# A fused attention and mixture-of-experts block on one core: row blocks turned by VectorE, expert weights split by ScalarE, gates folded into the shared expert, and another order at the end

## The chip, the cores and the metric

The kernel runs on one core of a Trainium2 chip as one launch. Its metric is the device time in microseconds; lower is better. A profile of one execution shows the engines by these names: PE (TensorE, with its weight loads as PEld), DVE (VectorE), ACT (ScalarE), POOL (GpSimd) and SP (SyncE, which issues most of the DMAs).

## The reference

Everything is float32. There are 32 sequences of 256 tokens with 128 features, 8192 tokens in all. Each sequence `b` has its own shift, scale and gate rows.

```
h = layernorm(x) * (1 + ca[b]) + sa[b]
x = x + ga[b] * attention(h)            # 16 heads of 64, softmax over the queries
h = layernorm(x) * (1 + cb[b]) + sb[b]
x = x + gb[b] * (routed(h) + shared(h) + 0.1 * anchor(h))
```

- `routed`: 32 experts of width 64 in 4 groups of 8. Every token takes the two groups with the highest group scores, and in them its 6 best experts; an expert computes `silu(h @ wg) * (h @ wu) @ wd`, weighted by the token's own weight for it.
- `anchor`: 16 small experts of width 32, four to a group; the token's best expert says which of them counts.
- `shared`: one expert of width 64 for all tokens.

## The kernel before

**Attention (the first 860 us).** The tokens are cut into 16 chunks of 512. A hand-written table says at which of the attention steps each portion of a chunk's norms and routing is dealt out. `through_dram` with `load_blocks` (L386 to L402) turns a normalized chunk: it is written to DRAM and read back in four DMAs of 32 columns each, after which one DVE transpose of 32x32 blocks (L652) completes the turn. Routing writes every token's row to DRAM twice, once for each of its two groups, by indirect DMAs of POOL (`route_send`, L850). A row is `ROW` = 180 floats: 128 features and 52 floats of weights.

**The passage to the experts (860 to 900 us).** SP issues the loads for the first expert tiles (`fetch_rows` for three tiles, `fetch_weights` for two, L1371 to L1374). Then a loop over seven pairs of chunks (L1379) computes the shared expert: `shared_up` (L1292) on PE, ACT and DVE, and one round later `shared_down` (L1305), whose two PSUM results are copied to `h2_all`, one by ACT and one by DVE. Between the rounds the routing of the last two chunks goes on, which takes DVE and POOL.

**The experts (900 to 1384 us).** There are 35 tiles of 512 tokens, each of one group. A tile `j` has five steps `k`: four pairs of routed experts and one step for the four anchors. In a step, `up` (L1237) does two PE products of 128x512 (`pg`, `pu`), `silu` on ACT and two DVE products, the first with `pu` and the second with the spread token weights `bt`; `down` (L1250) follows one step later with the product by `wd_sb` or `ad_sb` into one PSUM tile `py` for the tile. After a tile `send` (L1273) copies `py` on ACT and scatters it by four indirect DMAs of POOL to `y_d` in DRAM.

What a tile needs is prepared ahead by instructions dealt out between the steps (L1411 to L1420), in the program's order on every queue:

- `fetch_rows(j + 3)` and `fetch_weights(j + 2)` at `k == 0`: SP reads the tile's group and row from a table, and issues one DMA of rows and four of weights;
- `weights_mine(j + 2)` at `k == 1` on DVE; `weights_turn(j + 2)` at `k == 2`: a PE transpose (`pc`), an ACT copy (`cwt`), and on SP the DMA to DRAM (`cd`), followed at once by six DMAs that spread it over the partitions (`bt`, five slices of 512 columns);
- `rows_turn(j + 1)` at `k == 3`: four PE transposes (`ph`, L1233) and an ACT copy to `h`.

**The last sums.** When all of a chunk's tiles have been sent, `pass_load` (L1328) at `k == 4` loads its two shares and its gate row on SP. `pass_sum` four steps later adds the shares and the shared expert on DVE and multiplies by the gate on POOL; `pass_out` three steps after that adds `x1` and writes the chunk. The last shared pair is done inside the expert loop (L1429 to L1434). What is left over after the last tile runs at the end (L1443 to L1451); the last chunk goes there in two halves (`pass_rest`).

A tile waits in program order on its queue: an engine or SP that waits for one instruction does nothing that stands behind it.

Of the kernel before, what the change touches and what calls it, by code (L numbers as in the profile page):

```python
# [56 lines left out]
def adaln_block_kernel(  # L57
# [80 lines left out]
    def late_loads():  # L138

        nc.sync.dma_start(out=wd_sb, in_=w_down.rearrange("(k p) m -> p k m", p=P))  # L140
        nc.sync.dma_start(out=ad_sb, in_=an_down.rearrange("(k p) m -> p k m", p=P))
        nc.sync.dma_start(out=sg_sb, in_=sh_gate)
        nc.sync.dma_start(out=su_sb, in_=sh_up)
        for h in range(P // SI):
            nc.sync.dma_start(out=sd_sb[h * SI : (h + 1) * SI], in_=sh_down)
# [174 lines left out]
    with ExitStack() as actx:  # L320
# [516 lines left out]
        def route_write(c):  # L837

            w, ws, one = (chunk[c].pop(k) for k in ("w", "ws", "one"))
            meta = chunk[c]["rows"][:, :, D:].rearrange("p i (g w) -> p i g w", w=GW)  # L840
            wk = w.rearrange("p i (g k q) -> p i g k q", g=NG, q=2)
            for q in range(2):
                nc.gpsimd.tensor_tensor(
                    meta[:, :, :, q * EPG // 2 : (q + 1) * EPG // 2], wk[:, :, :, :, q],
                    ws.unsqueeze(2).unsqueeze(3).to_broadcast([P, NT, NG, EPG // 2]), ALU.mult,
                )
            pair = one.rearrange("p t (g l e) -> p t g l e", g=NG, e=2)
            nc.gpsimd.tensor_tensor(
                meta[:, :, :, EPG : GW - 1], pair[:, :, :, :, 0], pair[:, :, :, :, 1], ALU.add
            )  # L850
# [298 lines left out]
        fin = actx.enter_context(tc.tile_pool(name="fin", bufs=3, reuse_waits="tile"))  # L1149
# [9 lines left out]
        def fetch_rows(j):  # L1159
            t = T[j]  # L1160
            of, n = t["of"]
            t["g_sp"] = nc.sync.value_load(of.table[0:1, 0, n : n + 1], min_val=0, max_val=NG - 1)
            r = nc.sync.value_load(of.table[0:1, 1, n : n + 1], min_val=0, max_val=NG * SPAN)
            t["rw"] = rwp.tile([P, NT, ROW], F32, tag="rw", name=f"rw_{j}")
            got = nc.sync.dma_start(
                out=t["rw"],
                in_=rows_d[bass.ds(r, CH), :].rearrange("(p i) f -> p i f", i=NT),
            )
            if j < FIRST:
                tc.declare_no_dep(  # L1170
                    got.ins, group="late rows", reason="this tile holds rows of earlier chunks"
                )
                tc.add_to_no_dep_group("first tiles", got.ins)

        def fetch_weights(j):
            t = T[j]
            g = t.pop("g_sp")
            for key, src, srca in (("wg", w_gate, an_gate), ("wu", w_up, an_up)):
                w = wp.tile([P, KU + 1, P], F32, tag=key, name=f"{key}_{j}")
                nc.sync.dma_start(  # L1180
                    out=w[:, 0:KU, :].rearrange("p k f -> p (k f)"),
                    in_=src[:, bass.ds(g * (KU * P), KU * P)],
                )
                nc.sync.dma_start(out=w[:, KU, :], in_=srca[:, bass.ds(g * P, P)])
                t[key] = w

        def weights_mine(j):

            t = T[j]
            of, n = t["of"]  # L1190
            mm = mp.tile([P, NT, NG, GW], F32, tag="mm", name=f"mm_{j}", bufs=1)
            nc.vector.tensor_tensor(
                mm,
                t["rw"][:, :, D:].rearrange("p i (g w) -> p i g w", w=GW),
                of.mine[:, n, :].unsqueeze(1).unsqueeze(3).to_broadcast([P, NT, NG, GW]),
                ALU.mult,
            )
            m = mp.tile([P, GW, NT], F32, tag="m", name=f"m_{j}")
            nc.vector.tensor_reduce(m, mm.rearrange("p i g w -> p w i g"), AX.X, ALU.add)
            ix = mp.tile([P, NT], U32, tag="ix", name=f"iy_{j}", bufs=5)  # L1200
            nc.vector.tensor_copy(ix, m[:, GW - 1, :])
            t.update(m=m, ix=ix)

        def weights_turn(j):
# [10 lines left out]
            bt = bcp.tile([P, KU + 1, CH], F32, tag="bt", name=f"bt_{j}")  # L1215
            for q in range(2):
                nc.sync.dma_start(
                    out=bt[q * EI : (q + 1) * EI, 0:KU, :],
                    in_=cd[q * KU : (q + 1) * KU].partition_broadcast(EI),
                )  # L1220
            for q in range(NG):
                nc.sync.dma_start(  # L1222
                    out=bt[q * LI : (q + 1) * LI, KU, :],
                    in_=cd[2 * KU + q].partition_broadcast(LI),
                )
            t["bt"] = bt

        def rows_turn(j):
            t = T[j]
            rw = t.pop("rw")  # L1230
            ph = ps_mm.tile([P, CH], F32, tag="mm", name=f"ph_{j}")
            for i in range(NT):
                nc.tensor.transpose(ph[:, i * P : (i + 1) * P], rw[:, i, 0:D], ident)  # L1233
            t["h"] = mp.tile([P, CH], F32, tag="h", name=f"h_{j}", bufs=2)
            nc.scalar.copy(t["h"], ph)

        def up(j, k):  # L1237
            t = T[j]
            pg, pu = (
                ps_sc.tile([P, CH], F32, tag="sc", name=f"{n}_{j}_{k}") for n in ("pg", "pu")  # L1240
            )
            nc.tensor.matmul(pg, t["wg"][:, k, :], t["h"], start=True, stop=True)  # L1242
            nc.tensor.matmul(pu, t["wu"][:, k, :], t["h"], start=True, stop=True)  # L1243
            a = hid.tile([P, CH], F32, tag="a", name=f"a_{j}_{k}")
            nc.scalar.activation(a, pg, AF.Silu)  # L1245
            nc.vector.tensor_mul(a, a, pu)  # L1246
            nc.vector.tensor_mul(a, a, t["bt"][:, k, :])  # L1247
            return a

        def down(j, k, a):  # L1250
            t = T[j]
            of, n = t["of"]
            if k == 0:
                t["g"] = nc.tensor.value_load(
                    of.table[0:1, 0, n : n + 1], min_val=0, max_val=NG - 1
                )
                t["py"] = (
                    ps_av.tile([P, NT, D], F32, tag="av", name=f"py_{j}")
                    if j % 2
                    else ps_wo.tile([P, NT, D], F32, tag="po", name=f"py_{j}")  # L1260
# [6 lines left out]
            for i in range(NT):  # L1267
                nc.tensor.matmul(  # L1268
                    t["py"][:, i, :], a[:, i * P : (i + 1) * P], w,
                    start=k == 0 and i == 0, stop=k == KU and i == NT - 1,  # L1270
                )

        def send(j):  # L1273
            t = T[j]
            y = yp.tile([P, NT, D], F32, tag="y", name=f"y_{j}")
            nc.scalar.copy(y, t.pop("py"))  # L1276
            ix = t.pop("ix")
            for i in range(NT):
# [10 lines left out]
                tc.add_to_no_dep_group("y", sent.ins)  # L1289


        def shared_up(n):  # L1292
# [10 lines left out]
            return n, a  # L1303

        def shared_down(n, a, banks):  # L1305
# [5 lines left out]
            for i in range(NT):  # L1311
                for h in range(2):
# [6 lines left out]
                    )  # L1319
            for h, c in enumerate(cs):  # L1320
                (nc.scalar.copy, nc.vector.tensor_copy)[h](
                    h2_all[c], py[h].rearrange("p i d -> p (i d)")
                )
# [4 lines left out]
        def pass_load(c):  # L1328
            t = S_[c]
            t["s"] = [  # L1330
                xin.tile([P, NT, D], F32, tag="xt", name=f"s{k}_{c}") for k in range(2)
            ]
            for k, s in enumerate(t["s"]):
                o = k * B * S + c * CH
                got = nc.sync.dma_start(
# [3 lines left out]
            t["gate"] = fin.tile([P, BPC, D], F32, tag="gate", name=f"gate_{c}")  # L1339
            nc.sync.dma_start(  # L1340
                out=t["gate"],
                in_=gate_dram[c * BPC : (c + 1) * BPC].partition_broadcast(P),
            )

        def pass_sum(c):
            s0, s1 = S_[c]["s"]
            nc.vector.tensor_add(s0, s0, s1)
            nc.vector.tensor_add(s0, s0, h2_all[c].rearrange("p (i d) -> p i d", d=D))
            for b in range(BPC):
                nc.gpsimd.tensor_tensor(  # L1350
# [3 lines left out]
        def pass_rest(c, b):  # L1354
# [4 lines left out]
            nc.vector.tensor_add(  # L1359
                s0, s0, h2_all[c].rearrange("p (i d) -> p i d", d=D)[:, part]  # L1360
            )
# [17 lines left out]
        for n in range(PAIRS):  # L1379
# [12 lines left out]
            if n == 3:  # L1392
                weights_turn(1)
            if n == 4:
                rows_turn(0)
        shared_down(*prev, two_banks)
# [5 lines left out]
        prev = pair = None  # L1402
        for j in range(LISTS):
            for k in range(KU + 1):
                a = up(j, k)
                if prev is not None:
                    down(*prev)
                    if prev[1] == KU:
                        send(j - 1)
                prev = (j, k, a)  # L1410
# [6 lines left out]
                if k == 2 and j + 2 < LISTS:  # L1417
                    weights_turn(j + 2)
                if k == 3 and j + 1 < LISTS:
                    rows_turn(j + 1)  # L1420

# [7 lines left out]
                elif pair is None:  # L1429
                    assert FIRST - 3 > j  # L1430
                    pair = shared_up(PAIRS)
                elif len(pair) > 1:
                    shared_down(*pair, ((ps_mm, "mm"), (ps_mm, "mm")))
                    pair = (PAIRS,)  # L1434
# [3 lines left out]
                if k == 4 and started < NCH and complete[started] <= j:  # L1438
                    pass_load(started)
                    due[j + 1, 3] = lambda c=started: pass_sum(c)  # L1440
                    due[j + 2, 1] = lambda c=started: pass_out(c)
                    started += 1
        down(*prev)  # L1443
        send(LISTS - 1)
        for at in sorted(due):
            due[at]()
        for c in range(started, NCH):
            pass_load(c)
# [54 lines left out]
```

## Time and profile before

| | |
|---|---|
| median of 14 runs | 1406.59 us (1403.69 to 1411.37) |
| the profiled execution | 1405.5 us, of which 1403.7 us span |
| PE busy | 1349.7 us, 96% |
| DVE busy | 1015.8 us, 72% |
| ACT busy | 798.3 us, 57% |
| POOL busy | 767.6 us, 55% |
| mean granted TensorE clock | 0.988 |

The profile's page gives each engine's busy time, the span in 40 slices, and a chain of waits that is followed back from the last instruction. Further views give the instructions in order of time, the waits, and the busy time of each engine in a stretch. Busy times of an engine are averages over stages with different limits, so each stage is read by itself. Matmul durations are modelled from pipelined records: two that follow each other closely overlap in the list, so the distance between starts is the cost of one.

### The profile page before, as it was taken

The page shows a single profiled execution, that of the slowest core. Times are in us where ns is not written, and L with a number is a line of the kernel's source. Part 1 is how long each engine was busy: PE and PEld are TensorE (multiplying, and loading weights), DVE is VectorE, ACT ScalarE, POOL GpSimd, SP SyncE. Part 2 cuts the span into 40 slices and gives each one's busy share as a digit, 9 for nine tenths or more (in the row PEclk, how much of TensorE's full clock was granted, in tenths as well). Part 3 has the DMA queues.
Part 4 walks back from the last instruction along what each step waited for, and adds up shares of the span by engine and source line. Part 5 has one row for each costly group of instructions (what it writes and reads, how often), then busy time and mean ns, then how long its engine had stood idle before and what let it go on. Part 6 is the DMA issues. An engine that isn't in the chain of part 4 may idle for free. (4 is left out here: it accounts for less than half of the span.)

```text
span 1403.7 us, 33682 instructions
## 1 busy us (share of the span) xinstructions
PE 1349.7 (96%) x10543; PEld 841.6 (60%) x10543; DVE 1015.8 (72%) x4277; ACT 798.3 (57%) x2767; POOL 767.6 (55%) x1294
## 2 busy tenths in 40 slices
PE   6999999999999999999999998899999999999994
PEld 2566666666666666666666665456666666666662
DVE  5666888888888878888877776576656567766664
ACT  4777777777777777777777774223333333333331
POOL 3536467767767767767867646344323234343333
PEclk9999999999999999999999999999999999999997
DMA  4773622122022022022032014767667778878772
GB/s 154 275 264 116 221 75 50 42 75 62 31 75 62 30 75 62 30 75 62 31 75 47 33 48 118 191 175 214 179 181 199 193 206 231 266 223 256 227 210 63
DMA packets 183599, 182.50 MB, mean 130 GB/s; under 512 B 81520, under 2 KB 142656, under 8 KB 178944
## 3 DMA queue, kind: packets, MB, share of 16 engines
q1 hardware_dynamic: 172112, 159.62, 41.0%
q0 software_dynamic: 10624, 20.21, 4.3%
q8 instruction: 86, 1.41, 0.4%
q14 instruction: 89, 0.73, 0.2%
q10 hardware_dynamic: 688, 0.53, 0.1%
HBM read 121.37 MB, written 59.70 MB: 129 GB/s over the span
## 5 line engine op out<-in xcount | busy, mean ns | idle before, releaser
L549 ACT ACTIVATE e<-e,mn 128x256 f32<-128x256 f32 (+1 forms) x1024 | 453.5, 445 | 198.5 <-DVE mn L539 197.7
L539 DVE CUSTOM_DVE_ANT_0 e<-psc,mask 128x256 f32<-128x256 f32 (+1 forms) x1024 | 304.8, 344 | 4.4 <-PE psc L518 1.2
L1279 POOL DMA_INDIRECT y_d<-y,iy x140 | 137.9, 985 | 240.6 <-ACT y L1276 208.3
L568 POOL TENSOR_TENSOR vs<-v,rc 128x256 f32<-128x256 f32 x256 | 151.9, 616 | 212.0 <-DVE rc L557 199.9
L518 PEld LDWEIGHTS psc<-q,k 64*128 64x128 f32 x2048 | 166.2, 187 | 113.4 <-issue 101.6
L1246 DVE TENSOR_TENSOR a<-a,pu 128x512 f32<-128x512 f32 x175 | 120.1, 686 | 146.9 <-PE pu L1243 146.7
L1245 ACT ACTIVATE a<-pg 128x512 f32<-128x512 f32 x175 | 104.5, 597 | 183.0 <-PE pg L1242 174.9
L518 PE MATMUL psc<-q,k 64*128 64x256 f32 (+1 forms) x2048 | 202.1, 336 | 0.0
L586 PE MATMUL pav<-e,vs 128*64 128x256 f32 (+1 forms) x2048 | 195.1, 333 | 5.7 <-POOL vs L568 5.7
L549 ACT ACTIVATION_READ_ACCUMULATOR e<-e,mn 128x1 f32 x1024 | 192.7, 188 | 0.0
L1268 PEld LDWEIGHTS py<-wd_sb,a 128*128 128x128 f32 x1120 | 146.9, 192 | 70.3 <-issue 46.2
L1242 PE MATMUL pg<-h,wg 128*128 128x512 f32 x350 | 180.6, 598 | 0.0
L1243 PE MATMUL pu<-h,wu 128*128 128x512 f32 x350 | 179.6, 595 | 0.0
L468 PEld LDWEIGHTS po<-wo_sb,z 128*64 128x64 f32 x2048 | 121.8, 138 | 70.2 <-issue 69.7
L586 PEld LDWEIGHTS pav<-e,vs 128*64 128x64 f32 x2048 | 127.0, 136 | 58.5 <-POOL vs L568 6.4
L489 DVE TENSOR_SCALAR q<-pq,negbq 128x512 f32<-128x512 f32 x128 | 95.9, 749 | 76.9 <-PE pq L468 75.3
L856 POOL DMA_INDIRECT rows_d<-rows,ix x128 | 130.2, 1017 | 37.4 <-issue 34.6
L1268 PE MATMUL py<-wd_sb,a 128*128 x1120 | 148.2, 275 | 1.4 <-DVE a L1247 1.4
L479 DVE TENSOR_TENSOR v<-pv,bv_sb 128x512 f32<-128x512 f32 x128 | 88.3, 689 | 81.1 <-PE pv L468 79.7
L468 PE MATMUL po<-wo_sb,z 128*64 128x128 f32 x2048 | 134.7, 274 | 0.0
L468 PE MATMUL pq<-n_t,wqkv_sb 128*64 128x512 f32 x512 | 133.4, 600 | 0.7 <-ACT n_t L302 0.7
L468 PE MATMUL pv<-wqkv_sb,n_t 128*64 128x512 f32 x512 | 132.3, 596 | 0.8 <-DVE q L489 0.5
(239 smaller groups left out, 1770.6 us busy)
## 6 DMA issues: line engine op xcount, KB each, us to landing
bt<-cd SPq DMA_DIRECT2D x70, 512.0 KB
rows_d<-blank SPq DMA_DIRECT2D x69, 360.0 KB
rw<-rows_d SPq DMA_DIRECT2D x35, 360.0 KB
wg<-in_w_gate_dram SPq DMA_DIRECT2D x35, 256.0 KB
wu<-in_w_up_dram SPq DMA_DIRECT2D x35, 256.0 KB
bt<-cd SPq DMA_DIRECT2D x140, 64.0 KB
s<-y_d SPq DMA_DIRECT2D x32, 256.0 KB
mb<-mod_dram SPq DMA_DIRECT2D x31, 256.0 KB
```

The lines of the kernel that those rows point to most:

```text
L468: nc.tensor.matmul(ps[r], a[:, r], b, start=start, stop=stop)
L518: nc.tensor.matmul(pb[h][:, cols], k[r, o + kb * P : o + (kb + 1) * P], q[r, o + kb * P : o + S], start=True, stop=True,)
L539: nc.vector.tensor_tensor_reduce(e[:, cols], ps[:, cols], mask[:, cols], 1.0, 3e38, ALU.add, ALU.min, mn[:, b, kb, h : h + 1],)
L549: nc.scalar.activation(e[:, cols], e[:, cols], AF.Exp, bias=mn[:, b, kb, h : h + 1], scale=-1.0, accum_out=sm[:, b, kb, h : h + 1],)
L568: nc.gpsimd.tensor_tensor(vs[:, 2 * b : 2 * b + 2], vt[:, 2 * b : 2 * b + 2, col : col + P].rearrange("p k (h d) -> p k h d", h=2), rc[:, ...
L586: nc.tensor.matmul(pav[h * DH : (h + 1) * DH, o + kb * P : o + S], vs[:, 2 * b + kb, h, :], e[:, 0 : 2 * P] if kb == 0 else e[:, 2 * P : 3 ...
L856: sent = nc.gpsimd.indirect_dma_start(out=rows_d[:, :], out_offset=bass.IndirectOffsetOnAxis(ap=ix[:, k, i : i + 1], axis=0), in_=rows[:, ...
L1242: nc.tensor.matmul(pg, t["wg"][:, k, :], t["h"], start=True, stop=True)
L1243: nc.tensor.matmul(pu, t["wu"][:, k, :], t["h"], start=True, stop=True)
L1246: nc.vector.tensor_mul(a, a, pu)
L1268: nc.tensor.matmul(t["py"][:, i, :], a[:, i * P : (i + 1) * P], w, start=k == 0 and i == 0, stop=k == KU and i == NT - 1,)
L1279: sent = nc.gpsimd.indirect_dma_start(out=y_d[:, :], out_offset=bass.IndirectOffsetOnAxis(ap=ix[:, i : i + 1], axis=0), in_=y[:, i, :], in ...
```

## The change

- **Rows.** `fetch_rows` issues five DMAs in place of one: the 52 floats of weights, and the features in four blocks of 32 columns (`load_blocks`). `rows_turn` is one DVE transpose; the four PE transposes and the ACT copy are gone.
- **Weights.** The routed weights are loaded as they lie (`raw`), and `split_weights`, two ACT copies of 128x512 for each tile at `k == 2` and `k == 3`, put every fourth column together. With that the token weights of all four routed steps are the same slice, and `bt` has two slices in place of five.
- **Spread.** The DMAs to `bt` (five in place of six) are a function of their own, `weights_spread`, at `k == 4`.
- **Gates.** `shared_down` no longer copies: DVE multiplies each PSUM result by the gate row in two halves, and POOL adds it to `x1`. `shared_up` loads two gate rows on SP for it. `pass_sum` no longer adds the shared part, and the gate product (`pass_gate`) runs on DVE; the three steps of a chunk's last pass stand one tile later.
- **End.** The last tile is computed in two halves of 256 tokens, each sent by itself; the last shared pair comes behind the last tile; the last chunk's two loads are issued by ACT.

```diff
         def fetch_rows(j):
...
-            t["rw"] = rwp.tile([P, NT, ROW], F32, tag="rw", name=f"rw_{j}")
-            got = nc.sync.dma_start(
-                out=t["rw"],
-                in_=rows_d[bass.ds(r, CH), :].rearrange("(p i) f -> p i f", i=NT),
-            )
+            t["rw"] = rwp.tile([P, NT, ROW - D], F32, tag="rw", name=f"rw_{j}")
+            t["rh"] = rwp.tile([P, CH // BLK, BLK], F32, tag="rh", name=f"rh_{j}")
+            rows = rows_d[bass.ds(r, CH), :]
+            got = [
+                nc.sync.dma_start(
+                    out=t["rw"], in_=rows[:, D:].rearrange("(i p) f -> p i f", p=P)
+                ),
+                *load_blocks(t["rh"], rows),
+            ]
...
         def fetch_weights(j):
...
-                w = wp.tile([P, KU + 1, P], F32, tag=key, name=f"{key}_{j}")
+                raw = wp.tile([P, P, KU], F32, tag=f"{key}r", name=f"{key}r_{j}")
                 nc.sync.dma_start(
-                    out=w[:, 0:KU, :].rearrange("p k f -> p (k f)"),
+                    out=raw.rearrange("p f k -> p (f k)"),
                     in_=src[:, bass.ds(g * (KU * P), KU * P)],
                 )
-                nc.sync.dma_start(out=w[:, KU, :], in_=srca[:, bass.ds(g * P, P)])
-                t[key] = w
+                a = wp.tile([P, P], F32, tag=f"{key}a", name=f"{key}a_{j}")
+                nc.sync.dma_start(out=a, in_=srca[:, bass.ds(g * P, P)])
+                t[key] = raw, a
+
+        def split_weights(j, key):
+            t = T[j]
+            raw, a = t[key]
+            w = wp.tile([P, KU, P], F32, tag=key, name=f"{key}_{j}", bufs=2)
+            nc.scalar.copy(w, raw.rearrange("p f k -> p k f"))
+            t[key] = [w[:, k, :] for k in range(KU)] + [a]
...
-            bt = bcp.tile([P, KU + 1, CH], F32, tag="bt", name=f"bt_{j}")
-            for q in range(2):
-                nc.sync.dma_start(
-                    out=bt[q * EI : (q + 1) * EI, 0:KU, :],
-                    in_=cd[q * KU : (q + 1) * KU].partition_broadcast(EI),
-                )
+            t["cd"] = cd
+
+        def weights_spread(j):
+            t = T[j]
+            cd = t.pop("cd")
+            bt = bcp.tile([P, 2, CH], F32, tag="bt", name=f"bt_{j}")
+            nc.sync.dma_start(
+                out=bt[:, 0, :], in_=cd[0:EPG].unsqueeze(1).to_broadcast([EPG, P // EPG, CH])
+            )
             for q in range(NG):
...
         def rows_turn(j):
             t = T[j]
-            rw = t.pop("rw")
-            ph = ps_mm.tile([P, CH], F32, tag="mm", name=f"ph_{j}")
-            for i in range(NT):
-                nc.tensor.transpose(ph[:, i * P : (i + 1) * P], rw[:, i, 0:D], ident)
             t["h"] = mp.tile([P, CH], F32, tag="h", name=f"h_{j}", bufs=2)
-            nc.scalar.copy(t["h"], ph)
+            nc.vector.transpose(t["h"], t.pop("rh").rearrange("p x r -> p (x r)"))
...
+        def load_gate(c):
+            gate = fin.tile([P, BPC, D], F32, tag="gate", name=f"gate_{c}")
+            nc.sync.dma_start(
+                out=gate,
+                in_=gate_dram[c * BPC : (c + 1) * BPC].partition_broadcast(P),
+            )
+            return gate
...
-            return n, a
+            return n, a, [load_gate(c) for c in cs]
...
             for h, c in enumerate(cs):
-                (nc.scalar.copy, nc.vector.tensor_copy)[h](
-                    h2_all[c], py[h].rearrange("p i d -> p (i d)")
-                )
+                o = h2_all[c].rearrange("p (i d) -> p i d", d=D)
+                for b in range(BPC):
+                    nc.vector.tensor_tensor(
+                        tokens(o)[:, b], tokens(py[h])[:, b], by_batch(gates[h])[:, b], ALU.mult
+                    )
+                nc.gpsimd.tensor_tensor(x1_all[c], x1_all[c], o, ALU.add)
...
         def pass_sum(c):
             s0, s1 = S_[c]["s"]
             nc.vector.tensor_add(s0, s0, s1)
-            nc.vector.tensor_add(s0, s0, h2_all[c].rearrange("p (i d) -> p i d", d=D))
+
+        def pass_gate(c):
+            s0 = S_[c]["s"][0]
             for b in range(BPC):
-                nc.gpsimd.tensor_tensor(
+                nc.vector.tensor_tensor(
...
         for j in range(3):
             fetch_rows(j)
         for j in range(2):
             fetch_weights(j)
...
             if n == 3:
                 weights_turn(1)
+                weights_spread(0)
             if n == 4:
+                weights_spread(1)
                 rows_turn(0)
+            if n == 5:
+                split_weights(0, "wg")
+                split_weights(0, "wu")
...
         for j in range(LISTS):
-            for k in range(KU + 1):
-                a = up(j, k)
+            parts = [slice(0, NT)] if j < LISTS - 1 else [slice(0, NT // 2), slice(NT // 2, NT)]
+            for k, part in ((k, part) for part in parts for k in range(KU + 1)):
+                a = up(j, k, part)
...
+                if k in (2, 3) and j + 1 < LISTS:
+                    split_weights(j + 1, ("wg", "wu")[k - 2])
                 if k == 3 and j + 1 < LISTS:
                     rows_turn(j + 1)
+                if k == 4 and j + 2 < LISTS:
+                    weights_spread(j + 2)
...
-                elif pair is None:
-                    assert FIRST - 3 > j
-                    pair = shared_up(PAIRS)
-                elif len(pair) > 1:
-                    shared_down(*pair, ((ps_mm, "mm"), (ps_mm, "mm")))
-                    pair = (PAIRS,)
...
                     pass_load(started)
-                    due[j + 1, 3] = lambda c=started: pass_sum(c)
-                    due[j + 2, 1] = lambda c=started: pass_out(c)
+                    due[j + 2, 0] = lambda c=started: pass_sum(c)
+                    due[j + 2, 2] = lambda c=started: pass_gate(c)
+                    due[j + 2, 4] = lambda c=started: pass_out(c)
                     started += 1
+
+        pair = shared_up(PAIRS)
         down(*prev)
-        send(LISTS - 1)
+        send(LISTS - 1, prev[2])
+        shared_down(*pair, ((ps_mm, "mm"), (ps_mm, "mm")))
+        for c in range(started, NCH):
+            pass_load(c, nc.scalar)
         for at in sorted(due):
             due[at]()
-        for c in range(started, NCH):
-            pass_load(c)
```

Besides, `up`, `down` and `send` take the part of the tokens that they work on; routing writes its eight weights by one POOL product in place of two; the pool of gate rows has five buffers in place of three, and the shares have a pool of six buffers of their own.

## The prediction

> **What bounds the kernel now.** I read the busy time by stretches first, then the chain of waits, SP's queue in order of time, and the end. The stretches (length; busy us and instructions of each engine; clock; DMA share, GB/s):
>
> ```profile
> core 0: us, PE busy (x) PEld busy (x) DVE busy (x) ACT busy (x) POOL busy (x), PEclk, DMA share, GB/s
> 867.00:885.44 18.44, 17.36 (x150) 9.10 (x148) 17.00 (x75) 7.60 (x16) 9.12 (x24) 1.00 0.69 185
> 885.44:899.65 14.21, 8.46 (x47) 5.00 (x46) 7.39 (x20) 2.60 (x5) 5.26 (x7) 0.90 0.79 181
> 1000.00:1050.00 50.00, 50.00 (x240) 32.29 (x239) 29.45 (x49) 16.25 (x31) 14.79 (x16) 1.00 0.64 171
> 1252.00:1350.00 98.00, 94.39 (x448) 60.02 (x447) 65.01 (x108) 30.09 (x55) 38.26 (x40) 1.00 0.84 241
> 1375.00:1404.00 29.00, 8.25 (x43) 5.47 (x41) 11.37 (x20) 2.38 (x4) 9.49 (x10) 0.73 0.24 72
> ```
>
> In the experts PE is never idle from 1000 to 1250 us, and loses 3.6 us from 1252 to 1350. In the passage (867 to 885) DVE is busy for 92%. The chain shows one step of a tile and the transposes `ph` inside it:
>
> ```profile
> 1196.99 0.89 PE py L1268 x8
> 1197.88 0.44 PE ph L1233 x4
> 1198.32 0.86 PE pg L1242 x2
> 1199.18 0.86 PE pu L1243 x2
> 1200.04 0.89 PE py L1268 x8
> ```
>
> A step costs 0.86 + 0.86 + 0.89 = 2.61, a tile 5 x 2.61 + 0.44 (`ph`) + 0.11 (`pc`) = 13.60. SP's queue, at the start of the experts and late in them:
>
> ```profile
> 862.12 4.26 SPq L1165 DMA_DIRECT2D rw<-rows_d  x3
> 866.57 0.33 SPq L1180 DMA_DIRECT2D wg<-in_w_gate_dram  x1
> 867.09 0.33 SPq L1184 DMA_DIRECT2D wg<-in_an_gate_dram  x1
> ...
> 1226.31 0.45 SPq L1214 DMA_DIRECT2D cd<-cwt  x1
> 1230.68 1.10 SPq L1217 DMA_DIRECT2D bt<-cd  x2
> 1231.84 1.97 SPq L1222 DMA_DIRECT2D bt<-cd  x4
> 1235.24 0.32 SPq L1340 DMA_DIRECT2D gate<-gate_dram  x1
> 1238.23 0.35 SPq L1165 DMA_DIRECT2D rw<-rows_d  x1
> 1241.38 0.45 SPq L1214 DMA_DIRECT2D cd<-cwt  x1
> ```
>
> Late, SP needs 15.07 us from one `cd` to the next, more than PE's 13.60: it falls behind, `pass_sum` then waits for its shares in front of the steps' products, and that is where the 3.6 us go. The end:
>
> ```profile
> 1382.85 1.16 PE L1268 MATMUL py<-ad_sb,a 128*128 x8 [0.76 <-DVE a L1247]
> 1389.18 0.97 POOL L1279 DMA_INDIRECT y_d<-y,iy  x1 [0.30 <-issue]
> 1392.83 0.94 SPq L1335 DMA_DIRECT2D s<-y_d  x2
> 1399.63 0.43 DVE L1363 TENSOR_TENSOR s<-s,x 128x256 f32<-128x256 f32 x1
> ```
>
> **1. Rows turned by DVE: -15.0.** PE loses 0.44 a tile. Of 35 groups the first (876.63) lies in the passage, so 34 x 0.44 = 15.0. In exchange DVE gets one block transpose (L652: 0.71) at `k == 3`. A step's two products take 1.38 of DVE's 2.61; the extras are now at most one of 0.69 (`k == 0`, `k == 4`), 1.05 (`mm`, `m`, `iy`), 0.86 (gates, 2 x 0.43) or 0.71 a step. The fullest step is 1.38 + 1.05 = 2.43, so PE hides all of it; without that cover it would cost 0.71 a tile, 24 us in all.
>
> **2. Weights split by ACT: 0.** ACT loses the copy of `h` (0.59) and gets two copies of 128x512 that read every fourth float. No ACT row reads so. From below: the plain copy, 0.59. From above: DVE's strided reduction L1199, 0.51 for 208 elements, 1.26 for 512. I take 0.6 to 0.85, nearer to the row of the same engine. At `k == 2` ACT then holds 0.60 (`silu`) + 0.26 (`cwt`) + the copy; even 1.26 makes 2.12 of 2.61 and delays the next `silu` by some 0.7, against 0.9 between the end of a step's products and `down` (1364.01 to 1364.94). Beyond 1.5 us the excess counts twice a tile.
>
> The Trainium skill ("SBUF — State Buffer", at "Door 1: The DMA port swizzle") speaks against this copy: full speed needs consecutive hits in a 16-byte line, and this one takes a new line with each float. It gives no price; twice 0.59 would leave the sum as it is.
>
> **3. Shared pair out of the loop: -3.0.** Its products pushed two steps apart by 1.87 (993.57 to 995.44) and 1.09 (998.25 to 999.34).
>
> **4. The passage: +12.0.** SP, not the arithmetic, decides here. `fetch_rows` three times issues 12 more DMAs ahead of the weights, 0.52 each as the weight loads are spaced: +6.2, so the first weight goes out at 872.8 instead of 866.6. The eight weight loads take 4.2 more, to 877.0. Only then come the new gate rows of pair 0, landing at about 879.5 (2 to 2.5 us, as `hb_ln`, issued to 895.2 and used at 897.79). DVE meets the product with this gate where it copied `sy` at 867.00, and everything behind it waits: the next pair's `silu` product, routing of chunks 14 and 15, and PE, whose two banks stay full. POOL waits too: its adds stand ahead of chunk 13's last four sends. That is +12.5 (bounds +9 and +15, by the landing).
>
> Then DVE sets the pace up to the first `pg` (885.44): 17.00 busy, less 6 copies of 0.69, plus 24 gate products at 0.36 (L628, from PSUM: 0.71 for two), plus 0.71 for the first transpose, gives 22.2, at the old 92% to 95% about 23.5 instead of 18.44: +5.
>
> Given back: behind the first `pg` PE stood still for 5.75 us for the logits of chunk 15, since `hd_ln` (888.15) was queued behind `bt`; and the clock was 0.90 in that stretch, a pair of `pg` taking 2.08 instead of 1.02. In the new order SP is past `bt` by then, and what is left is POOL's chain: six adds of about 1.42 each (twice L383's 0.71) ahead of chunk 15's norm. I put the rest of the stall at 2: -3.5 there, -2 for the slow matmuls. 12.5 + 5 - 3.5 - 2 = +12.0; bounds +5 and +18.
>
> On the clock, the Trainium skill ("TensorE: Matmul & The Clock Gate", Part 1: The HAM clock gate) says that an idle window of some 3.4 us halves it for as long again. By it the new hole costs half of 3.4, an estimate of 1.7 us, beneath DVE's rounds; no part of the sum uses it.
>
> **5. Stalls late in the experts: -3.6, and SP: +1.5.** `pass_sum` stands two steps and a tile after its load instead of four steps, 15.7 us instead of 10.4, so its waits go. What is late next is SP's cycle: four more row DMAs (+2.1), one large spread fewer (-0.58): 15.07 becomes 16.6 with the same 4.37 from `cd` to `bt`. That wait was 1.49 at 1046.09, when DMA was idler. The spread falls from 1280 to 512 KB a tile, the row blocks move as many features as before; at 860 us, with such blocks, the DMA moved 205 GB/s at a share of 0.95, against 388 at 1208. So I take 2.2, a cycle of 14.4, nearer to the idle row. Against PE's 13.16 that is 1.2 a tile over the eleven tiles in a row that load shares, 13.6, less some 2 us of SP's idle time and 7.5 us of lead (15.7, less 2.2 from the step to the issue and 6 for landing, `s` in the chain: 6.17): 4 at worst, nothing at a cycle of 14; I take 1.5.
>
> **6. The end: -3.5.** Two sends behind the last product instead of four: 2 x 1.28 = 2.6. ACT issues the two loads without SP's wait for chunk 14's output (0.5); each half is added with three products instead of four, 2 x 0.43. Against it: the last pair's `sg` and `su` (1.87) stand before the last `down`, of which some 1.3 were waiting time: +0.5. Its five DVE products, two adds behind the sends on POOL, and two chunks' last passes (2 x 2.2 on DVE) end before the last shares land, 3.5 after their issue; if not, they cost up to 2. In the half tiles a step has 1.31 on PE, DVE 0.85: hidden. Routing's one POOL product less a chunk lies beside attention, as does the new order of `wd_sb` in its load: 0.
>
> **Sum.** -15.0 - 3.0 + 12.0 - 3.6 + 1.5 - 3.5 = -11.6: 1393.9 against the profiled 1405.5, which is 1.1 below the median; as a median 1395.0, own range 1389 to 1402.
>
> **Rivals.**
> - *The gates are no hold-up* (17%): they land before DVE asks, or the stalls behind absorb the shift; the passage costs nothing. 1383. For it: the 5.75 us of idle PE. Against it: the order on SP.
> - *SP becomes the bound, slower than before* (11%): the place is the eleven tiles from the seventeenth on, the price 16.6 - 13.16 = 3.4 a tile, 37 less 9.5 of lead: 1395 - 1.5 + 28 = 1421.5. It decides from a cycle of 15.4 (`cd` to `bt` 3.2). For it: that wait was 4.37. Against it: 768 KB a tile less.
> - *The strided copy is slow* (5%): at 1.7 us, 0.2 x 2 x 34 = 13.6: 1409.
> - *The change doesn't do what it says* (7%): DVE's transpose makes `a` late, 0.2 a tile: 1402.
> - Forecast: 60%.
>
> Faster by over 0.2% (about what a measurement can tell from no change): 60 + 17 + 5 = 0.82; within it 0.06; slower 0.12. From 1381 to 1407 some 17% is left out.
>
> **What would show it.** Starts of `py` 13.16 apart per tile between 1000 and 1200; PE idle for some 13 us near 868 to 881, DVE there waiting for the DMA of `gate`; first `pg` near 903; `cd` to `cd` below 14.5 late; the strided copy at 0.6 to 0.85; two sends and loads on ACT's queue at the end. I am wrong where DVE does not wait for the gate, or PE waits for `bt`, the shares or the split weights.

## The result, and the profile after

The changed kernel takes 1418.04 us (median of 11 runs, 1413.12 to 1420.04) against 1409.32 us of the kernel before (median of 52 runs): ratio 1.0063, 95% interval 1.0051 to 1.0076, so slower by 0.6%. Its profiled execution has a span of 1416.4 us, 12.7 above that of before, where the forecast had 11.6 less.

Where the difference lies is read from the starts of a few products in PE's order of time; `sg` is the first shared product, `py n` the first output product of tile n:

| from | to | before | after | difference | predicted |
|---|---|---|---|---|---|
| start | `sg` | 859.6 | 860.4 | +0.8 | 0 |
| `sg` | `py 1` | 52.1 | 81.1 | **+29.1** | +12.0 - 0.4 |
| `py 1` | `py 7` | 89.5 | 84.5 | -5.0 | -3.0 - 6 x 0.44 |
| `py 7` | `py 24` | 231.1 | 223.7 | -7.4 | -17 x 0.44 |
| `py 24` | `py 33` | 127.4 | 125.7 | -1.7 | -9 x 0.44 - 3.6 + 1.5 |
| `py 33` | last `py` | 24.0 | 25.2 | +1.2 | end: |
| last `py` | end | 20.0 | 15.7 | -4.3 | -3.5 together |

Two rows are wrong: the passage by 17.5 us, the tiles late in the experts by 4.4. The stretches of the changed kernel (columns as in the prediction: length, then busy us and instructions of PE, PEld, DVE, ACT, POOL, then clock, DMA share, GB/s):

```profile
core 0: us, PE busy (x) PEld busy (x) DVE busy (x) ACT busy (x) POOL busy (x), PEclk, DMA share, GB/s
862.00:884.00 22.00, 7.32 (x50) 2.92 (x48) 2.74 (x6) 2.90 (x5) 2.93 (x3) 0.76 0.72 158
884.00:917.00 33.00, 22.89 (x139) 12.42 (x139) 26.93 (x91) 5.14 (x9) 26.30 (x37) 0.70 0.38 97
...
1020.00:1070.00 50.00, 50.00 (x233) 31.84 (x232) 33.55 (x57) 20.84 (x34) 15.57 (x16) 1.00 0.56 141
1252.00:1350.00 98.00, 93.69 (x431) 58.56 (x430) 70.43 (x122) 40.99 (x64) 28.59 (x29) 1.00 0.67 183
```

In the 22 us from 862 on PE works for a third of the time, DVE, ACT and POOL for an eighth. In the 33 us behind it DVE is busy for 82% and POOL for 80% (before, from 867 to 885, 92% and 49%). From 1020 to 1070 PE is full, and late it still loses 4.3 us. The first hole stands in SP's queue:

```profile
864.51 0.42 SPq L1169 DMA_DIRECT2D rw<-rows_d  x1
...
875.20 0.36 SPq L1186 DMA_DIRECT2D wgr<-in_w_gate_dram  x1
...
879.75 5.34 SPq L1313 DMA_DIRECT2D gate<-gate_dram  x6
```

The gate rows go out at 879.75, behind fifteen row and eight weight DMAs. On DVE (in brackets, idle time ahead of the instruction and what ended it):

```profile
869.30 0.69 DVE L1330 TENSOR_TENSOR sa<-sa,su 128x512 f32<-128x512 f32 x1 [3.17 <-PE su L1325]
883.99 1.42 DVE L1352 TENSOR_TENSOR h<-sy,gate 128x256 f32<-128x256 f32 x4 [14.00 <-DMA gate<-gate_dram]
885.32 0.85 DVE L681 TENSOR_SCALAR sig<-th 128x128 f32<-128x128 f32 x1
...
897.96 0.17 DVE L700 TENSOR_TENSOR mid<-hi 128x16 f32<-128x16 f32 x1
898.05 1.25 DVE L701 TENSOR_TENSOR lo<-lo 128x16 f32<-128x16 f32 x1
...
907.06 0.22 DVE L809 COPY m<-m 128x24 f32<-128x24 f32 x1 [3.12 <-POOL m L805]
...
912.36 0.69 DVE L1330 TENSOR_TENSOR sa<-sa,su 128x512 f32<-128x512 f32 x1 [1.16 <-PE su L1325]
```

DVE stands 14.00 us for the gate, as forecast. What was not forecast is below it: an operation of 16 elements a partition takes 1.25 us where its neighbour takes 0.17, and DVE waits 3.12 us for a POOL memset, later 1.16 for PE. POOL at that time, and then PE:

```profile
896.73 2.53 POOL L1355 TENSOR_TENSOR x<-x,h 128x512 f32<-128x512 f32 x2 [1.52 <-DVE h L1352]
...
904.42 2.48 POOL L1355 TENSOR_TENSOR x<-x,h 128x512 f32<-128x512 f32 x2
...
906.90 0.12 POOL L805 MEMSET m<- 128x32 f32 x1
...
907.04 1.04 POOL L753 TENSOR_TENSOR cnt<-cnt,gm 128x4 f32<-128x4 f32 x4
```

```profile
898.51 1.08 PE L1325 MATMUL sg<-h,sg_sb 128*64 128x512 f32 x4
...
908.13 0.41 PE L471 MATMUL pr<-cnt,ones 128*64 128x20 f32 x4 [4.31 <-POOL cnt L753]
...
908.58 1.96 PE L1325 MATMUL sg<-h,sg_sb 128*64 128x512 f32 x4
```

The add to `x1` at 896.73 covers the 1.25 us operation of DVE; that at 904.42 stands ahead of the memset and of `cnt`, for which PE waited 4.3 us. Behind that wait PE ran at half its clock (granted 0.50 from 905 to 914), and the same four products took 1.96 us in place of 1.08. Late in the experts, SP, then ACT, then DVE, then PE:

```profile
1307.99 0.37 SPq L1229 DMA_DIRECT2D cd<-cwt  x1
1311.36 0.67 SPq L1237 DMA_DIRECT2D bt<-cd  x1
...
1321.57 0.35 SPq L1186 DMA_DIRECT2D wgr<-in_w_gate_dram  x1
...
1323.71 0.37 SPq L1229 DMA_DIRECT2D cd<-cwt  x1
```

```profile
1325.62 1.12 ACT L1199 COPY wg<-wgr 128x512 f32<-128x512 f32 x1 [2.82 <-DMA wgr<-in_w_gate_dram]
```

```profile
1304.49 0.69 DVE L1375 TENSOR_TENSOR s<-s,s 128x512 f32<-128x512 f32 x1 [2.97 <-DMA s<-y_d]
```

```profile
1306.56 1.16 PE L1288 MATMUL py<-wd_sb,a 128*128 x8 [1.34 <-DVE a L1266]
...
1328.73 1.16 PE L1288 MATMUL py<-wd_sb,a 128*128 x8 [1.95 <-DVE a L1266]
```

The raw weights go out at 1321.57, ACT's split waits 2.82 us for them, the next `silu` stands behind the split, and PE waits 1.95 us for `a`. One of PE's four late waits has another origin: at 1304.49 `pass_sum` holds DVE for 2.97 us until its shares have landed, the products of the step stand behind it, and PE waits 1.34 us. The end:

```profile
1402.97 0.97 POOL L1299 DMA_INDIRECT y_d<-y,iy  x1 [0.30 <-issue]
1403.71 3.30 DVE L1375 TENSOR_TENSOR s<-s,s 128x512 f32<-128x512 f32 x1
1403.96 2.50 POOL L1355 TENSOR_TENSOR x<-x,h 128x512 f32<-128x512 f32 x2
1405.10 0.84 ACTq L1367 DMA_DIRECT2D s<-y_d  x2
...
1412.87 0.42 DVE L1390 TENSOR_TENSOR s<-s,x 128x256 f32<-128x256 f32 x1
```

Two sends and ACT's loads are as forecast; the DVE add of 0.69 takes 3.30 beside POOL's last two adds.

### The profile page after: what moved, and what is told of

Its sections match the earlier page's. It is cut to its first block, busy times and chain, and to the rows that moved or that the text cites. A ratio compares the mean times of both kernels' runs of the same rounds, so it can differ in the third digit from the quotient of the medians.

```text
span 1416.4 us, 33957 instructions
## 1 busy us (share of the span) xinstructions
PE 1344.8 (95%) x10423; PEld 832.9 (59%) x10423; DVE 1052.2 (74%) x4359; ACT 842.7 (59%) x2800; POOL 762.4 (54%) x1264
## 4 chain that ended last, share of the span: by engine, by line
PE 83%; DVE 5%; issue 3%; POOL 3%; DMA 3%; SPq 2%; ACT 0%; DVEq 0%; POOLq 0%; ACTq 0%
PE psc L521 13%; PE pav L589 12%; PE py L1288 9%; PE pg L1260 8%; PE pu L1260 8%; PE pv L471 8%; PE pq L471 8%; PE pk L471 7%; PE po L471 7%; SPq L395 1%; POOL rows_d L856 1%; DVE a L1265 1%; PE psc L471 1%; DVE e L542 1%; DVE a L1266 1%
## 5 line engine op out<-in xcount | busy, mean ns | idle before, releaser
L1264 ACT ACTIVATE a<-pg 128x512 f32<-128x512 f32 (+1 forms) x180 | 105.3, 585 | 187.7 <-PE pg L1260 183.4
L1265 DVE TENSOR_TENSOR a<-a,pu 128x512 f32<-128x512 f32 (+1 forms) x180 | 120.9, 672 | 119.3 <-PE pu L1260 80.5
L1260 PE MATMUL pg<-h,wg 128*128 128x512 f32 (+1 forms) x288 | 145.3, 586 | 0.0
L1260 PE MATMUL pu<-h,wu 128*128 128x512 f32 (+1 forms) x288 | 144.5, 584 | 0.0
```

Of the source, the lines that this page charges most:

```text
L1260: nc.tensor.matmul(ps[:, cols], t[key][k], t["h"][:, cols], start=True, stop=True)
L1264: nc.scalar.activation(a[:, cols], pg[:, cols], AF.Silu)
L1265: nc.vector.tensor_mul(a[:, cols], a[:, cols], pu[:, cols])
```

## The experiments

**Theory A**: of the excess in the passage one part is the hold (gate rows behind rows and weights on SP), another POOL's adds. Rivals: **B**, the adds alone decide, and **C**, the later rows and weights alone. In the first session the kernel before took 1416.16 us, and in 20 to 22 of the 35 tiles of each kernel ACT's `cwt` started 0.6 us or more, mostly 1.3 to 1.4, after the end of PE's `pc` (0.08 in the other sessions); a tile took 13.7 us where the same kernel later took 13.16. So the four kernels were run once more, and the numbers used are the second ones. Of the two texts below each edit the first was written for the first session, the second for the second.

**Gate rows on ACT's queue.** In `shared_up`; `load_gate` takes the queue, and `pass_load` leaves it at SP:

```diff
-            return n, a, [load_gate(c) for c in cs]
+            return n, a, [load_gate(c, nc.scalar) for c in cs]
```

> The changed kernel, but the gate rows of the shared pairs are issued on ACT's queue, so they do not stand behind the rows and weights on SP's queue. Theory A (the hold: DVE's gate product waited 17.0 us for a DMA that stands behind 15 row DMAs and 8 weight loads): the 14.0 us wait of DVE goes, PE's 12.3 us hole goes, the first gate product comes near 868 instead of 884; 14 to 17 us faster than the changed kernel, 1401 to 1404. Theory B (POOL's adds to x1 are the brake, at 1.25 us each, ahead of the routing's own POOL work, and DVE slows beside them): the hole goes, but the rounds behind it stay long, first pg of tile 0 near 908 instead of 916.9; about 8 us faster, 1410. Theory C (the rows and weights themselves, later on SP by 12 DMAs): next to nothing, 1416 to 1418, because tile 0 waits for its weights or rows instead.

> The changed kernel with the pairs' gate rows issued on ACT's queue, once more on another chip. Theory A (hold and adds each cost about half): the 12 us hole of PE goes, the rounds stay slow; first shared product to first pg 42 to 46 us in place of 56; 9 to 14 us faster than the changed kernel, ratio 0.996 to 1.000. Theory B (behind the hold the adds would have taken the time anyway): less than 5 us faster, ratio over 1.002.

The 17.0 us in the first text are not DVE's wait for the gate, which is 14.00; ahead of all its gate products together DVE idled for 16.9.

**Adds dealt out later.** In `shared_down` and in the loop over the tiles (what is left over is added at the end):

```diff
-                nc.gpsimd.tensor_tensor(x1_all[c], x1_all[c], o, ALU.add)
+                adds.append(
+                    lambda c=c, o=o: nc.gpsimd.tensor_tensor(x1_all[c], x1_all[c], o, ALU.add)
+                )
...
+                if k == 2 and j >= 3 and adds:
+                    adds.pop(0)()
```

> The changed kernel, but POOL's fourteen adds of the gated shared part to x1 are dealt out one a tile from the fourth expert tile on, so none stands in the passage. Theory A: the hold stays (DVE's first gate product near 884), behind it the rounds shorten by what the adds cost, 5 to 9 us: 1409 to 1413. Theory B: the rounds go at DVE's pace of 23 us or less, first pg near 905: 12 us faster, 1406; DVE's short operations beside the adds go back from 0.85 to 1.25 us to their 0.2. Theory C: no change, 1416 to 1418.

> The changed kernel with POOL's adds dealt out one a tile in tiles 3 to 16, once more on another chip. Theory L (DVE's products of two SBUF operands stand still while POOL's add runs: a times bt took 2.42 instead of 0.69 beside the add, a times pu, which reads PSUM, stayed at 0.68): first shared product to first pg 45 to 48 instead of 56, but the tiles with an add take 13.6 to 14.0, those without 13.16, so that the total is within 3 us of the changed kernel, ratio 1.004 to 1.008. Rival (the chip alone made the tiles long): all tiles 13.16, 9 us faster, ratio 1.000.

**Both edits.**

> Both at once: gate rows on ACT's queue and POOL's adds dealt out later. Theory A and B together: the whole excess of the passage goes but for the later weights, first pg of tile 0 at 888 to 895; 22 to 27 us faster than the changed kernel, 1391 to 1396. Theory C: 1412 or more, with PE waiting for weights or rows at tile 0.

> Both, once more on another chip. Theory A with L: first shared product to first pg 33 to 36 us; tiles with an add 13.6 to 14.0; 10 to 15 us faster than the changed kernel, ratio 0.996 to 1.000. What is left against the kernel without the folding in the passage, 5 to 7 us, is the gate rows' place in the queues and DVE's longer products.

**Folding undone.** Besides what is shown, the pairs load no gate rows, and `pass_rest` adds the shared part to each half of the last chunk:

```diff
-                for b in range(BPC):
-                    nc.vector.tensor_tensor(
-                        tokens(o)[:, b], tokens(py[h])[:, b], by_batch(gates[h])[:, b], ALU.mult
-                    )
-                nc.gpsimd.tensor_tensor(x1_all[c], x1_all[c], o, ALU.add)
+                (nc.scalar.copy, nc.vector.tensor_copy)[h](
+                    h2_all[c], py[h].rearrange("p i d -> p (i d)")
+                )
...
             nc.vector.tensor_add(s0, s0, s1)
+            nc.vector.tensor_add(s0, s0, h2_all[c].rearrange("p (i d) -> p i d", d=D))
```

> The changed kernel without the folding of the gates: shared_down copies as before (one ACT, one DVE copy), no gate rows are loaded for the pairs, the shared part is added to the shares in pass_sum on DVE. All the rest of the change stands. Theories A and B: as with both removed, first pg near 888 to 893, 1390 to 1396; the late stalls (7.3 us in tiles 28 to 31) stay, as DVE's extra add of 0.69 lies beside PE. Theory C: 1412 or more.

> The changed kernel without the folding of the gates, once more on another chip: on the first one PE's signals reached ACT 1.4 us late in most tiles, and the changed kernel's control on another chip had 13.16 a tile. From first shared product to first pg of tile 0: 27 to 29 us (changed kernel 56, before 26 to 29); tiles 13.16; the stalls late in the experts stay at 5 to 11. 27 to 31 us faster than the changed kernel, ratio 0.984 to 0.989. If the folding's cost were half given back later: 0.995.

In the first session the ratios to the kernel before were 1.0059 (gates on ACT), 1.0106 (adds later), 1.0019 (both) and 0.9943 (folding undone). Theory A's times (1390 to 1413 us) were all missed there, with 1423.83, 1430.82, 1419.67 and 1407.82. In the second, with the passage divided at `sy`, the first output product of the second shared pair, and at `pg`, the first product of tile 0:

| kernel | `sg` to `sy` | `sy` to `pg` | `pg` to `py 1` | ratio to before |
|---|---|---|---|---|
| before (two profiles) | 9.1, 12.0 | 16.7, 16.7 | 26.2, 25.1 | 1 |
| after | 24.5 | 32.0 | 24.7 | 1.0063 |
| gates on ACT | 9.7 | 30.6 | 24.1 | 0.9965 [0.9944, 0.9985] |
| adds later | 23.7 | 21.7 | 23.3 | 1.0081 [1.0055, 1.0107] |
| both | 14.9 | 20.8 | 24.7 | 0.9975 [0.9946, 1.0004] |
| folding undone | 12.4 | 17.5 | 19.5 | 0.9862 [0.9832, 0.9892] |

The two causes separate by columns. With the gates on ACT's queue the first column returns to that of before (9.7; in "both" only to 14.9), and the second stays; with the adds gone the second loses 10 us, and the first stays. The first session's profiles divide in the same way (first two columns: gates on ACT 15.1 and 31.1, adds later 26.1 and 21.7, both 12.6 and 22.6, folding undone 11.8 and 19.0). So A holds, and B alone is out: the hold is worth 9 to 15 us, the adds 10. The ratios of the second session are those that A expected ("adds later" at the upper edge); of the times from `sg` to `pg` two fell just outside, 40.3 for 42 to 46 with the gates on ACT, and 29.9 for 27 to 29 with the folding undone. C is out: with the folding undone, rows and weights still go out as late (first weight at 875.41, 875.20 after), and `pg` still comes 29.9 us after `sg`, against 25.8 and 28.7 before and 56.5 after.

How the adds cost these 10 us is read from the stretch `sy` to `pg`, first after, then with the adds later (columns as above):

```profile
884.89:916.90 32.01, 22.79 (x138) 12.29 (x138) 25.94 (x89) 5.14 (x9) 26.14 (x37) 0.70 0.37 94
```

```profile
885.14:906.82 21.68, 18.98 (x138) 10.66 (x139) 20.95 (x92) 5.18 (x9) 8.02 (x22) 0.88 0.42 110
```

DVE's busy time falls from 25.94 to 20.95, by 5.0; its idle time falls from 6.07 to 0.73, by 5.3. The idle time after is 3.12 for the memset `m`, which stands behind two adds, and 1.16 and 1.24 for PE, which had stood 4.31 for `cnt` in the same queue and then worked at half its clock (with the adds later the clock is 1.00 from 892 on). The next stretch, from `pg` to `py 1`, first before, then after:

```profile
885.44:911.68 26.24, 20.48 (x90) 12.10 (x90) 11.68 (x27) 6.43 (x12) 5.92 (x8) 0.87 0.80 195
```

```profile
916.90:941.57 24.67, 21.25 (x87) 12.37 (x86) 15.06 (x33) 7.30 (x12) 9.83 (x11) 0.86 0.52 129
```

PE's work takes 0.8 us more at a clock that is as low as before, and PE idles 2.3 less.

The adds dealt out later did not get cheaper, only moved. From the eighth tile on, those with an add took 14.02, those without 13.16. One add in the kernel with the adds later, first POOL's line, then DVE's:

```profile
1091.44 1.31 POOL L1356 TENSOR_TENSOR x<-x,h 128x512 f32<-128x512 f32 x1
```

```profile
1090.16 0.69 DVE L1265 TENSOR_TENSOR a<-a,pu 128x512 f32<-128x512 f32 x1
1090.89 2.43 DVE L1266 TENSOR_TENSOR a<-a,bt 128x512 f32<-128x512 f32 x1
1093.24 0.67 DVE L1265 TENSOR_TENSOR a<-a,pu 128x512 f32<-128x512 f32 x1
```

`a` times `bt` takes 2.43 us in place of 0.69, and ends 0.57 after the add. In this run it overlapped an add 14 times and took 0.93 to 2.43, and a median of 0.69 in the other 156 cases; the product with `pu`, which reads PSUM, overlapped one three times and stayed at 0.68 to 0.69. So the lengthening comes from POOL's operation, not from more work on DVE. The Trainium skill ("SBUF — State Buffer", at "SBUF: two separate sides") says that a GpSimd operation and a DVE operation with two SBUF inputs, or in a two-port mode, take one pair of ports by turns, each for its whole length, and that the other stands still. The runs agree: an operation of two SBUF inputs stood still, the gate products from PSUM (0.41 in ten overlaps) did not; one with a single SBUF input (L681, 0.85 against 0.22) did too, as the page has it for the two-port mode, which the trace does not name. `MATCH_REPLACE8` (0.18) and `TENSOR_REDUCE` (0.29) beside an add kept their length. How the turn is decided these runs don't show: in all fourteen cases the product ended 0.55 to 0.56 us after the add, though in eleven its record starts 0.23 to 0.58 ahead of the add's.

Moving the gates to ACT had a price of its own. SP's queue in that kernel:

```profile
873.53 6.12 SPq L395 DMA_DIRECT2D rh<-rows_d  x4
879.84 0.36 SPq L1186 DMA_DIRECT2D wgr<-in_w_gate_dram  x1
884.52 0.36 SPq L1191 DMA_DIRECT2D wga<-in_an_gate_dram  x1
```

```profile
881.38 0.93 ACTq L1313 DMA_DIRECT2D gate<-gate_dram  x2
```

Four row DMAs take 6.12 us to issue instead of 1.94, and the second weight goes out 4.7 behind the first (0.6 in the changed kernel). A semaphore is the counter by which a landed DMA is announced. In this trace the DMAs of SP and ACT use eight semaphores in turn, and each waits until the one before it on its semaphore has landed: here `wga` of tile 0 has the semaphore of a gate row that ACT issues only at 881.38. A second queue did not make the loads independent. From `sg` to `py 1` "both" stays 11 us behind the folding undone (2.5, 3.3 and 5.2 in the three columns); how much of that the shared semaphores cost was not tried.

**Controls**, both kernels as they are, in a session between those two:

> The changed kernel as it is, once more, beside the kernel before on the same chip: the four experiments ran on a chip where the kernel before took 1416 us, and a tile of theirs took 13.7 to 14.0 us between 1010 and 1200 us where the changed kernel's profile has 13.16. Theory A (another chip or hour, where signals between engines come later): here too a tile takes 13.16 or 13.7 and the ratio to the kernel before stays at 1.006; Theory B (moving the gates or adds out of the passage brings the loss into the tiles): the tiles take 13.16, ratio 1.006.

> The kernel before as it is, for its profile on this chip. Ratio 1.000. If the chip is what lengthened the tiles, a tile takes more than 13.60 between 1010 and 1150 us wherever the tiles of the other runs of this call are longer too.

After: ratio 1.0064 [1.0042, 1.0086], tiles 13.16; before: 1.0003 [0.9987, 1.0020], tiles 13.60. The tiles of 13.7 in the first session do not belong to the kernels; those of 14.02 do, as they came back. Late in the experts, from `py 24` to `py 33`, the control of the changed kernel lost more than its first profile: 11.4 us over nine tiles of 13.16, where that lost 7.3.

**Spread one step later.** Theory S and its rivals concern the tiles late in the experts:

```diff
-                if k == 4 and j + 2 < LISTS:
-                    weights_spread(j + 2)
+                if k == 0 and 0 < j and j + 1 < LISTS:
+                    weights_spread(j + 1)
```

> The changed kernel, but the spread of a tile's token weights is issued one step later, at k == 0 of the next tile behind its row and weight loads, so that SP's wait from cd to bt (2.9 us of a cycle of 14.7) lies beside other issues. Theory S (late in the experts SP's cycle of 14.7 is over PE's 13.16, so the raw weights come late, ACT's split waits for them, silu stands behind the split): the cycle falls below 13.2, the 7.2 us of stalls in tiles 28 to 31 go, 6 to 7 us faster than the changed kernel. Rival (the loads land late for lack of DMA bandwidth): the stalls stay, no change. Rival (the spread itself becomes late): PE waits at the first step of each tile for bt, 5 us or more slower.

Ratio 1.0006 [0.9989, 1.0022], 7.4 us less than the changed kernel in the same session, and every tile from the eighth to the 33rd takes 13.16. SP's queue now:

```profile
1284.21 0.37 SPq L1229 DMA_DIRECT2D cd<-cwt  x1
...
1294.05 0.35 SPq L1186 DMA_DIRECT2D wgr<-in_w_gate_dram  x1
...
1296.13 0.67 SPq L1237 DMA_DIRECT2D bt<-cd  x1
...
1298.77 0.36 SPq L1229 DMA_DIRECT2D cd<-cwt  x1
```

The spread goes out right behind the weights, with no wait of its own. The stalls are gone, so it was SP's order; the rivals (bandwidth, a late spread) are out. From 1205.93 to 1322.82 nine cycles take 12.99 on average, below PE's 13.16, so SP falls behind no more.

**No folding, and the spread later.**

> The changed kernel without the folding of the gates and with the spread issued one step later. If both causes are what they seem and independent: 17 us (as without the folding) plus 6 us faster than the changed kernel, ratio to the kernel before 0.988 to 0.991. If SP's lag late is bandwidth: 0.994 as without the folding alone.

1380.81 us, ratio 0.9805 [0.9776, 0.9833]: the fastest of all, 28 us under the kernel before, and better than expected. The two edits add up: 0.0201 and 0.0057 below the changed kernel's 1.0063 would be 0.9805.

## Why the prediction was wrong

1. **Rows turned by DVE, -15.0: right.** A tile takes 13.16 instead of 13.60, in every tile without a stall; DVE's transpose is hidden.
2. **Split copies, 0: the sum right, the size not.** A copy takes 1.12 us, not 0.6 to 0.85, but less than the 1.5 from which it counts, and 13.16 shows that it costs nothing while the weights are there. The rule of the skill that was weighed (a new 16-byte line with each float) spoke in the right direction: 1.12 against 0.59 for the plain copy. But the plain copies of this size read PSUM and the split reads SBUF; no run separates the stride from the source.
3. **Shared pair out of the loop, -3.0: right**; 2.4 by the table (5.0 less 6 x 0.44).
4. **The passage, +12.0: this step failed.** Of its terms:
   - *The hold, +12.5*: right, 12.5 to 15.4 against before. The weights went out at 875.20 rather than 872.8, the gate rows at 879.75, and they took 4.2 us to land, not 2 to 2.5.
   - *DVE sets the pace, +5*: this is the term that was mis-sized; from `sy` to `pg` it measured 15.3. DVE's own longer products are 4 to 5 of it, since the kernel with the adds later takes 21.7 there (17.5 with the folding undone, 16.7 before); a gate product took 0.41, not 0.36. The other 10.3 are POOL's adds, which the prediction put on POOL alone and charged only ahead of chunk 15's norm. By the stretches above, half of this is DVE operations that get longer beside an add (those listed by the trace come to some 6 us), and half is DVE waiting for what stands behind the adds in POOL's queue: for `m` directly, for `cnt` by way of PE.
   - *Given back, -5.5*: only 0.4 to 1.5 came back. The stall shrank as forecast, from 5.75 to 1.73 us (forecast: 2), but two waits of 0.92 and 0.78 came up, and PE's slow matmuls stayed: its work took 0.8 more, not 2 less. Without the folding the wait for the logits is the same (1.78), and the stretch takes 19.5 us at a clock of 1.00 (21.2 at 0.92 in the two other profiles without it). The adds alone are not the reason, since with the adds later it takes 23.3, and 24.7 in "both". Why the clock stays low in this stretch was not tried.
   - *The clock in the hole*, which no part of the sum used: it stood at 0.50 from 877 to 893, longer than the 3.4 us behind the estimate of 1.7. In DVE's rounds it cost little: with the adds later, `sy` to `pg` takes 21.7 with the hold (clock 0.88) and 20.8 without it (1.00).
5. **Late in the experts, -3.6 + 1.5: the mechanism of the second rival, mis-sized.** SP was the next limit, as forecast. But its cycle was 14.72 (1161.84 to 1323.71, eleven tiles), not 14.4, with 3.0 on average from `cd` to `bt` (2.4 to 4.3), not 2.2. The prediction's own formula gives (14.72 - 13.16) x 11 - 9.5 = 7.7; the tiles lost 125.7 - 9 x 13.16 = 7.3. That the two are so close is luck, as the same kernel's control lost 11.4. Nor did `pass_sum`'s waits go, as -3.6 had it: one of PE's four waits (1.34 of 5.4) still comes from the shares, the other three from the raw weights at ACT's split; `bt` did not hold PE. With the spread one step later, and so with SP in time, both kinds are gone.
6. **The end, -3.5: right**, 1.2 - 4.3 = -3.1.

None of the rivals was the outcome. "The gates are no hold-up" fell with DVE's 14.00 us, and SP as the bound cost 7 us, not 28. What was missing was a rival in which POOL's new work slows DVE; the prediction gave 0.12 to slower.

## What to carry to other kernels

Work that is handed to POOL can cost DVE time: look for the DVE operations that will run beside it, those with two operands from SBUF first (here one product lost up to 1.74 us beside an add of 1.3, one with an operand from PSUM nothing), and for what stands behind it in POOL's own queue. A load added to a long queue goes out behind everything issued ahead of it, as the gate rows did behind 23 DMAs, and a second queue helps only as far as no shared semaphore ties it to the first. Where one engine's cycle per tile is close to another's, the bounds of a few tenths of a microsecond have to be carried times the number of tiles into the range; and an edit bundled of several parts should be judged part by part, since here one part cost 28 us and hid the gain of the others.

## What the runs showed of the hardware

- A DVE product of two SBUF operands (128x512) took 2.43 us beside a POOL add of 1.3, 0.69 alone; a 128x16 operation 1.25 instead of 0.17.
- ACT's copy that gathers every fourth float from SBUF took 1.12 us for 128x512, a plain one from PSUM 0.59.
- In one session of three, each on another chip, ACT's `cwt` started 0.6 us or more after the end of PE's `pc` in 20 to 22 of 35 tiles, mostly 1.3 to 1.4 (0.08 elsewhere), in all four kernels of that session. Why is open: `cwt` waits for PE, but for a DMA's semaphore too. It went with tiles of 13.7 us in place of 13.16.
- After PE had stood 4.31 us, it worked at a granted clock of 0.50 from 905 to 914: four products took 1.96 us in place of 1.08.
